# Order of the loads and of the second layer's preparation at the head of a Mamba and attention megakernel

## Chip, cores and metric

The kernel runs on one core of one Trainium2 chip. The metric is the time of one execution on the device in microseconds (us); lower is better. Everything is fp32.

## The reference, cut to what matters

The program is a chain of four image layers on x of shape (2, 128, 64, 64). The change touches the first layer and the preparation for the second.

```python
def layer0(x, ...):                       # two Mamba + FFN blocks over 4096 tokens of 128 channels
    t = tokens(embed_w @ x + embed_b)
    for i in range(2):
        r = t
        t2 = layernorm(t, ln_g[i], ln_b[i])
        u, z = split(t2 @ in_w[i].T)
        u = silu(causal_conv4(u, conv_w[i]) + conv_b[i])
        dt, Bm, Cm = split(u @ xproj_w[i].T)
        dt = softplus(dt @ dtproj_w[i].T + dtproj_b[i])
        A = -exp(A_log[i])                # (256, 16)
        # h_t = exp(dt*A) * h_{t-1} + dt*u*Bm ;  y_t = h_t . Cm + u*ssm_D
        t = ((y * silu(z)) @ mout_w[i].T) + r
        t = t + ffn(layernorm(t))         # gelu FFN, 4x wide
    return x + outc_w @ t + outc_b
# layer 1: q, k, v by 3x3 convolutions, softmax attention over 4096 positions, 1x1 convolution, + x
# layer 2: attention with 1x1 q, k, v;  layer 3: 3x3 convolutions at four scales, attention over the scales
```

## The kernel before

**The tiling.** Layer 0 is cut into 32 items: image b (2) times block l (2) times chunk c (8 chunks of 512 tokens). Each item has 8 steps (`NST`) of the scan, each step holds 4 state rows for 128 partitions, and a period of 32 slots (`NSL`) belongs to each item. The loop at L514 runs over periods i = -2 to 33. In each slot it issues, in a fixed order, the scan of item i with what feeds it (`spread_dt`, `spread_dtu`, `y_pair`, `scan`, `decay`, `times_b`, L350 to L402) and then what `background(i)` has listed for the slot (L463): for item i+2 the embedding and first layer norm, for item i+1 the projection (`pu_taps`, `xproj`, `spread_bc`, `dtproj`, `soft_plus`), for items i-1 and i-2 the output and the FFN. Periods -2 and -1 have no scan of their own: they fill the pipeline.

**What sets the order.** The order is written out by hand: each engine runs its instructions in the order in which the program issues them (`tc.manual_schedule`). SyncE (SP) issues nearly all DMAs in this order on one queue. DMA completions are counted on eight semaphores used in turn, so an issue also waits until the DMA eight places before it has landed.

**The head.** SP issues, in this order: `kc` (constants, L76), `vec` (L77), the eight chunks of image 0 (L93), `we` (embedding weights, L121), then for both blocks `wl` (L139), `cw` in two parts (L141 the four convolution taps spread over all partitions, L142 the input projection), and `wd` (L144), then the three `raw` convolution weights of layer 1 (L163) and the eight chunks of image 1 (L166).

The other engines prepare both blocks one after the other (L146 to L159): four VectorE (DVE) products `wu` of the projection with each tap (L148), `an = -exp(A_log)` on ScalarE (ACT) and DVE (L150, L151), and four TensorE (PE) matmuls `pa` (L155) that spread `an` over partitions, each followed by four small DVE copies into `am` (L158). Only then does period -2 begin with `embed` of chunk 0 (L213).

`pa` takes its PSUM from the pool `mm` (two buffers, L114), as do `pe`, `pc`, `var`, `pr`, `pu`, `pd`, `pt` and others. `pu` of one half keeps its buffer from its first tap (slot 0 of the period) to `pu_out` (slot 2).

**Period -1** (around the change): `pu_taps` for item 0 at slots 0, 1, 3 and 4 (four taps for each half of the 256 inner channels, two in each slot), `fold(k)` for k = 0, 1, 2 at slots 2, 10 and 18 (L490), `silu` at slot 11, `xproj` 13, `spread_bc` 14, `soft_plus` 17, the first `spread_dt` at slot 20. `fold` (L168) is ten DVE operations that make transformed weights for layer 1 out of `raw`, and two DMA stores to `ufold` in DRAM (L184), which are read again only after layer 0. `cw`, `raw`, `ulo`, `uhi` and the scan's `h` share one tag of five SBUF buffers.

`spread_bc` (L323) stores rows of `dbl` to DRAM (L326) and reads them back spread over partitions, as `bb` and `cb`, 256 KB in each of eight DMAs (L331). `spread_dt` (L350) makes `dtb` for one step with four DMAs of 64 KB (L355); `decay` (L368) needs it, and `scan` (L375) needs `decay`.

Of the kernel before, what the change touches and what calls it, by code (L numbers as in the profile page):

```python
# [6 lines left out]
F32 = mybir.dt.float32  # L7
AF = mybir.ActivationFunctionType
ALU = mybir.AluOpType
# [4 lines left out]
B, C, H, W = 2, 128, 64, 64  # L14
N = H * W
P = 128
CH = 512
NCH = N // CH
RPC = CH // W
NL = 2  # L20
DS = 16
DI = 2 * C
# [3 lines left out]
KC = 4  # L26
# [41 lines left out]
def tile_conv_seq(ctx: ExitStack, tc, x, consts, vecs, wemb, wlay, wconv, wdt, wqkv, wsmall, wms, out):  # L68
    nc = tc.nc
# [9 lines left out]
    def xv(b, c):  # L79

        return xt[:, b, 1 + c * RPC : 1 + (c + 1) * RPC, 1 : W + 1]
# [7 lines left out]
        nc.gpsimd.memset(xt[:, b, 1 : H + 1, 0:1], 0.0)  # L89
        nc.gpsimd.memset(xt[:, b, 1 : H + 1, W + 1 : W + 2], 0.0)  # L90

    for c in range(NCH):
        nc.sync.dma_start(xv(0, c), x[0, :, c * RPC : (c + 1) * RPC, :])  # L93

    ud = ctx.enter_context(tc.tile_pool(name="ufold", bufs=1, space=bass.MemoryType.DRAM))
    ufold = [ud.tile([P, 18, C], F32, name=f"ufold{k}") for k in range(3)]
# [14 lines left out]
    with ExitStack() as s, tc.manual_schedule():  # L111
        wp = s.enter_context(tc.tile_pool(name="l0w", bufs=1))
        sp = s.enter_context(tc.tile_pool(name="l0s", bufs=1))
# [18 lines left out]
        def four(g):  # L132
            return fsel[:, g].rearrange("p q d -> p (q d)")

        nc.scalar.preload_act_table_set(EXP_LN_SET)
        wl, wu, wd, am = [], [], [], []
        for l in range(NL):
            w = wp.tile([P, NWL - DI], F32, name=f"wl{l}")
            nc.sync.dma_start(w, wlay[l][:, DI:])  # L139
            cw = sp.tile([P, KC + 1, DI], F32, name="cw", tag="h", bufs=5)  # L140
            nc.sync.dma_start(cw[:, :KC, :].rearrange("p k d -> p (k d)"), wconv[l : l + 1, :].to_broadcast([P, KC * DI]))  # L141
            nc.sync.dma_start(cw[:, KC, :], wlay[l][:, :DI])  # L142
            d = wp.tile([R, DI], F32, name=f"wd{l}")
            nc.sync.dma_start(d, wdt[l])  # L144

            u = wp.tile([P, KC, DI], F32, name=f"wu{l}")  # L146
            for k in range(KC):
                nc.vector.tensor_tensor(u[:, k, :], cw[:, KC, :], cw[:, k, :], ALU.mult)  # L148
            an = wp.tile([P, NJ * DS], F32, name=f"an{l}")
            nc.scalar.activation(an, vec[:, VEC[f"A_log{l}"] : VEC[f"A_log{l}"] + NJ * DS], AF.Exp)  # L150
            nc.vector.tensor_scalar(an, an, -1.0, None, ALU.mult)  # L151
            a = wp.tile([P, NJ, 4, 4], F32, name=f"am{l}")
            for g in range(4):
                pa = mm.tile([P, NJ, DS], F32, name="pa", tag="mm")
                nc.tensor.matmul(pa.rearrange("p j n -> p (j n)"), lhsT=four(g), rhs=an, start=True, stop=True)  # L155
                for q in range(4):
                    at = slice(32 * q, 32 * q + 32)
                    nc.vector.tensor_copy(a[at, :, g, :], pa[at, :, 4 * q : 4 * q + 4])  # L158
            wl.append(w), wu.append(u), wd.append(d), am.append(a)  # L159
        raws = []  # L160
        for which in range(3):
            raw = sp.tile([P, 3, 3, C], F32, name="raw", tag="h", bufs=5)
            nc.sync.dma_start(raw.rearrange("p y x c -> p (y x) c"), wqkv[:, which])  # L163
            raws.append(raw)
        for c in range(NCH):
            nc.sync.dma_start(xv(1, c), x[1, :, c * RPC : (c + 1) * RPC, :])  # L166

        def fold(which):  # L168

# [26 lines left out]
        def has(i):  # L196
            return 0 <= i < NI
# [265 lines left out]
        def background(i):  # L463

            todo = [[] for _ in range(NSL)]

            def at(t, f, *a):
                todo[t].append((f, a))

            n, p, q, r = i + 1, i - 1, i - 2, i + 2  # L470
            if has(q):
                at(3, gelu, q)
                at(6, ffn_down, q, (0, 1)), at(7, ffn_down, q, (2, 3)), at(9, ffn_add, q)
                at(11, out_mm, q), at(12, out_add, q)
            if has(p):
                at(7, y_out, p, 1), at(7, gate, p)
                at(9, mix_out, p), at(11, mix_add, p)
            if has(n):
                at(0, pu_taps, n, 0, (0, 1)), at(1, pu_taps, n, 0, (2, 3)), at(2, pu_out, n, 0)
                at(3, pu_taps, n, 1, (0, 1)), at(4, pu_taps, n, 1, (2, 3)), at(5, pu_out, n, 1)  # L480
                at(13, xproj, n), at(14, xproj_out, n), at(14, spread_bc, n)
                at(15, dtproj, n, 0), at(16, dtproj, n, 1), at(17, soft_plus, n), at(18, dt_end, n)
            if has(i):
                at(1, pz_mm, i, 0), at(3, pz_out, i, 0)
                at(5, pz_mm, i, 1), at(6, pz_out, i, 1)
            if has(i) or has(n):
                at(11, silu, i, n)
            if i == -1:
                for k in range(3):
                    at(8 * k + 2, fold, k)  # L490
            pair = [(k, second) for k, second in ((p, True), (r, False)) if has(k)]
            if has(r):
                at(10, embed, r), at(11, embed_out, r)
            w, m = {}, len(pair)
            for k, (it, second) in enumerate(pair):
                at(12 + 2 * k, ln_centre, w, k, it)
                at(13 + 2 * k, ln_square, w, k, it)
                at(27, ln_spread, w, k, m), at(28, ln_scale, w, k, it)
                at(29, ln_shift, w, k, it, second)
            if pair:  # L500
                at(17, ln_var, w, m), at(18, ln_eps, w, m), at(19, ln_rs, w, m), at(20, ln_newton, w, m), at(21, ln_step, w, m)
            if has(p):
                for f in range(4):
                    at(30 + f // 2, ffn_up, p, f)
            if has(i):
                at(24, y_out, i, 0)
            return todo
# [6 lines left out]
        for i in range(-2, NI + 2):  # L514
            todo = background(i)
            for t_ in range(NSL):
                t = i * NSL + t_
                g, m = divmod(t, 4)
                if m == 0 and 0 <= g + 3 < NG:
                    spread_dt(g + 3)  # L520
                if m == 0 and 0 <= g + 1 < NG:
                    spread_dtu(g + 1)
                if m == 0 and g % 2 == 1 and 0 <= g - 3 < NG:
                    y_pair(g - 3)
                if 0 <= t < NT:
                    scan(t)
                if 0 <= t + 4 < NT:
                    decay(t + 4)
                if m == 3 and 0 <= g + 1 < NG:
                    times_b(g + 1)  # L530
                for f, a in todo[t_]:
                    f(*a)
# [14 lines left out]
    with ExitStack() as s, tc.manual_schedule():  # L547
        sp = s.enter_context(tc.tile_pool(name="ats", bufs=1))
# [259 lines left out]
        for now in range(NALL + LAG + 10):  # L808
            r, u = divmod(now, NU)
            w = now % 8  # L810
# [56 lines left out]
    with ExitStack() as s, tc.manual_schedule():  # L867
        sp = s.enter_context(tc.tile_pool(name="mss", bufs=1))
# [50 lines left out]
        for si in (2, 3):  # L919
            wgt[si] = sp.tile([P, SCALES[si]], F32, name=f"wgt{si}")  # L920
            for k in range(SCALES[si]):
                w = (k + 0.5) / SCALES[si] - 0.5
# [398 lines left out]
```

## Time and profile before

| | |
|---|---|
| median of 3 runs | 5102.76 us |
| lowest, highest | 5097.54, 5103.26 us |
| profiled execution, its own time | 5104.57 us |
| its span | 5102.8 us |
| mean granted TensorE clock | 0.946 |
| PE, DVE, ACT, POOL busy | 92%, 80%, 46%, 45% of the span |
| first embedding matmul (`pe`, L213) | 28.91 us after the span's start |
| first projection matmul (`pu`, L288) | 46.34 us |
| first `dtb` DMA issued (L355) | 74.15 us |
| first scan (L384) | 84.72 us |

Times in the views are counted from the start of the span. "DMA x<-y" in the chain of waits is the time from an issue to its landing; "issue" is time in which the engine waited for nothing that the profile shows. SPq is SyncE's queue. PEld is TensorE's loading of weights. A matmul of the program is two instructions on PE in fp32, so "x16" for `pu` is eight taps.

### The profile page before, as it was taken

The page shows a single profiled execution, that of the slowest core. Times are in us where ns is not written, and L with a number is a line of the kernel's source. Part 1 is how long each engine was busy: PE and PEld are TensorE (multiplying, and loading weights), DVE is VectorE, ACT ScalarE, POOL GpSimd, SP SyncE. Part 2 cuts the span into 40 slices and gives each one's busy share as a digit, 9 for nine tenths or more (in the row PEclk, how much of TensorE's full clock was granted, in tenths as well). Part 3 has the DMA queues.
Part 4 walks back from the last instruction along what each step waited for, and adds up shares of the span by engine and source line. Part 5 has one row for each costly group of instructions (what it writes and reads, how often), then busy time and mean ns, then how long its engine had stood idle before and what let it go on. Part 6 is the DMA issues. An engine that isn't in the chain of part 4 may idle for free.

```text
span 5102.8 us, 48990 instructions
## 1 busy us (share of the span) xinstructions
PE 4686.2 (92%) x14797; PEld 2249.2 (44%) x14797; DVE 4094.2 (80%) x4416; ACT 2367.7 (46%) x3221; POOL 2317.8 (45%) x1948
## 2 busy tenths in 40 slices
PE   5888899899888998789999999999999998999997
PEld 1222222222222222256666666666666666333332
DVE  5999999999999999588888887667766775667775
ACT  4677777777777777412222232333333332323332
POOL 2777777666777777313332233333333332322331
PEclk8899998998999989899999999999999999999998
DMA  5333333332333333124443344444444443000000
GB/s 150 73 68 68 70 71 72 71 70 68 69 69 68 69 71 72 36 53 104 101 105 82 78 100 105 118 95 112 111 99 97 112 111 76 3 7 5 7 8 7
DMA packets 237016, 373.86 MB, mean 73 GB/s; under 512 B 88000, under 2 KB 88400, under 8 KB 228432
## 3 DMA queue, kind: packets, MB, share of 16 engines
q1 hardware_dynamic: 187600, 303.55, 25.0%
q10 hardware_dynamic: 49152, 67.17, 5.5%
q8 instruction: 118, 1.93, 0.2%
q14 instruction: 146, 1.20, 0.1%
HBM read 92.18 MB, written 9.83 MB: 20 GB/s over the span
## 4 chain that ended last, share of the span: by engine, by line
PE 46%; POOL 21%; DVE 13%; issue 11%; DMA 4%; ACT 3%; SPq 3%; DVEq 0%; ACTq 0%; POOLq 0%
POOL h L387 17%; PE po L756 13%; PE pq L706 13%; DVE tr L736 3%; DMA pt<-tr 2%; SPq L747 2%; PE pf L1008 2%; PE py L399 2%; PE pqkv L1035 2%; PE pw L1094 1%; POOL dtu L347 1%; POOL z L410 1%; PE pfus L1159 1%; PE pu L288 1%; PE psc L1059 1%
## 5 line engine op out<-in xcount | busy, mean ns | idle before, releaser
L743 POOL COPY pt<-tr 32x512 f32<-32x512 f32 x1024 | 657.8, 642 | 1496.0 <-DVE tr L736 769.0
L384 DVE TENSOR_TENSOR_SCAN h<-da,carry,h 128x512 f32<-128x512 f32 x1024 | 1240.9, 1265 | 60.1 <-ACT da L373 29.9
L387 POOL TENSOR_TENSOR h<-h,cb 128x2048 f32<-128x2048 f32 x256 | 1161.0, 4535 | 20.9 <-POOL carry L386 0.2
L706 PE MATMUL pq<-k,q 128*128 128x512 f32 x2048 | 966.5, 595 | 11.0 <-DVE sc L711 8.7
L756 PE MATMUL po<-pt,vt 128*128 128x256 f32 x4096 | 965.6, 379 | 2.5 <-DMA pt<-tr 2.5
L721 ACT ACTIVATE sc<-sc,nm 128x2048 f32<-128x2048 f32 x256 | 510.6, 1995 | 938.9 <-DVE nm L717 651.9
L711 DVE TENSOR_SCALAR_CACHE_REDUCE sc<-pq 128x1024 f32<-128x1024 f32 x512 | 625.0, 1222 | 361.3 <-PE pq L706 339.7
L756 PEld LDWEIGHTS po<-pt,vt 128*128 128x128 f32 x4096 | 777.9, 190 | 294.8 <-issue 211.4
L373 ACT ACTIVATE da<-dtb,am 128x512 f32<-128x512 f32 x1024 | 681.6, 684 | 223.8 <-DVE h L384 212.0
L736 DVE STREAM_TRANSPOSE tr<-sc 128x2048 f32<-128x2048 f32 x256 | 591.7, 2311 | 68.3 <-DMA pt<-tr 61.4
L366 DVE TENSOR_TENSOR h<-bb,pdu 128x2048 f32<-128x2048 f32 x256 | 581.3, 2271 | 78.4 <-PE py L399 29.4
L399 PE MATMUL py<-h,sel 128*32 128x512 f32 x2048 | 512.1, 644 | 1.6 <-POOL h L387 1.6
L706 PEld LDWEIGHTS pq<-k,q 128*128 128x128 f32 x2048 | 384.4, 191 | 291.3 <-issue 248.0
L360 PE MATMUL pdu<-dtu,fsel 128*128 128x512 f32 x512 | 324.3, 719 | 104.3 <-DVE h L366 104.2
L399 PEld LDWEIGHTS py<-h,sel 128*32 128x32 f32 x2048 | 115.4, 118 | 415.0 <-issue 407.9
L288 PE MATMUL pu<-xn,wu 128*128 128x512 f32 x512 | 246.1, 614 | 4.1 <-ACT xn L278 2.3
L360 PEld LDWEIGHTS pdu<-dtu,fsel 128*128 128x128 f32 x512 | 95.6, 213 | 309.8 <-DVE h L366 190.5
L386 POOL COPY carry<-h 128x4 f32<-128x4 f32 x256 | 47.8, 187 | 390.3 <-DVE h L384 386.4
L1101 DVE TENSOR_TENSOR ov<-v,pw 128x2048 f32<-128x2048 f32 x64 | 146.2, 2285 | 68.6 <-PE pw L1094 68.6
L1035 PE MATMUL pqkv<-f,ws 128*128 128x512 f32 x384 | 189.5, 618 | 3.0 <-DVE prod L1052 2.3
L1105 POOL TENSOR_TENSOR ov<-ov 128x2048 f32<-128x2048 f32 x16 | 72.6, 4537 | 257.6 <-DVE ov L1101 257.6
L261 PE MATMUL pr<-rs,kc 2*128 2x512 f32 (+1 forms) x128 | 90.2, 834 | 77.3 <-POOL rs L257 71.1
(241 smaller groups left out, 5331.8 us busy)
## 6 DMA issues: line engine op xcount, KB each, us to landing
pt<-tr SPq DMA_DIRECT2D x2048, 64.0 KB, 2.0
dtb<-dt SPq DMA_DIRECT2D x1024, 64.0 KB, 2.0
pt<-tr ACTq DMA_DIRECT2D x1024, 64.0 KB, 2.2
bb<-dr SPq DMA_DIRECT2D x128, 256.0 KB, 4.6
cb<-dr SPq DMA_DIRECT2D x128, 256.0 KB, 7.5
uw<-ufold SPq DMA_DIRECT2D x14, 576.0 KB, 3.9
xt<-in_x SPq DMA_DIRECT2D x16, 256.0 KB, 5.0
xr<-in_x SPq DMA_DIRECT2D x16, 256.0 KB, 2.9
```

Source lines behind the costliest of these rows:

```text
L360: nc.tensor.matmul(pdu, lhsT=four(s_ % 4), rhs=st[i]["dtu"][:, s_ // 4, :], start=True, stop=True)
L366: nc.vector.tensor_tensor(h, st[i]["bc", 0], pdu.unsqueeze(1).to_broadcast([P, 4, CH]), ALU.mult)
L373: nc.scalar.activation(da, st[i]["dtb", s_], AF.Exp, scale=am[items[i][1]][:, j, gg, m : m + 1])
L384: nc.vector.tensor_tensor_scan(h[:, m, :], da, h[:, m, :], carries[b, l][:, j, gg, m : m + 1], ALU.mult, ALU.add)
L387: nc.gpsimd.tensor_tensor(h, h, st[i]["bc", 1], ALU.mult)
L399: nc.tensor.matmul(py[r : r + 32, :], lhsT=sel, rhs=st[i]["h", s_ + k][:, m, :], start=(m == 0), stop=(m == 3), tile_position=(0, r),)
L706: nc.tensor.matmul(pq[:, i, :], lhsT=st["q", r, grp][:, it * P : (it + 1) * P], rhs=st["k"][:, at : at + CH], start=True, stop=True)
L711: nc.vector.tensor_scalar(dst, pq, 1.0, None, ALU.mult, ALU.max, accum_out=st["mx"][:, c2 : c2 + 1])
L721: nc.scalar.activation(sc, sc, AF.Exp, bias=nm, scale=scale, accum_out=sm[:, hh : hh + 1])
L736: nc.vector.transpose(tr, st.pop(("sc", r, blk, hh)).rearrange("p (t r f) -> p r t f", r=NB, f=32))
L743: nc.gpsimd.tensor_copy(dst, src)
L756: nc.tensor.matmul(st["po", r, grp], lhsT=st["vt"][:, jt, :], rhs=rhs, start=(jt == 0), stop=(jt == N // P - 1))
```

## The change

At the head, the loads are put in the order of use: `kc`, `vec`, `we`, chunk 0 of image 0, block 0's weights with `cw` first, then chunks 1 to 7 of image 0, block 1's weights, `raw`, image 1. Block 1's preparation (`prepare(1)`: `an`, the four `pa` with their copies, and the four products `wu`) moves out of the head to slot 0 of period -1, where it is issued just after the first two taps of `pu` for item 0. The loads of `raw` and of image 1 are issued from slot 1 of period -1, and `fold` moves from slots 2, 10, 18 to 6, 14, 22. Inside `prepare`, `an` and `am` come before `wu`. Nothing else differs, and no operation is added or removed.

On SP, the order of instructions differs in two places only: the loads at the head, and in period -1, where the two stores of `fold(1)` now stand after `cb` and ahead of the first `dtb`, and those of `fold(2)` between the four DMAs of the first `dtb` and those of the second. Before, `fold(0)` and `fold(1)` stood ahead of `dr`, and `fold(2)` between `cb` and the first `dtb`.

```diff
-    for c in range(NCH):
-        nc.sync.dma_start(xv(0, c), x[0, :, c * RPC : (c + 1) * RPC, :])
+    def load_x(b, c):
+        nc.sync.dma_start(xv(b, c), x[b, :, c * RPC : (c + 1) * RPC, :])
...
         nc.scalar.preload_act_table_set(EXP_LN_SET)
-        wl, wu, wd, am = [], [], [], []
-        for l in range(NL):
+        load_x(0, 0)
+        wl, wu, wd, am, cws = [], [], [], [], []
+
+        def load_layer(l):
+            cw = sp.tile([P, KC + 1, DI], F32, name="cw", tag="h", bufs=5)
+            nc.sync.dma_start(cw[:, KC, :], wlay[l][:, :DI])
+            nc.sync.dma_start(cw[:, :KC, :].rearrange("p k d -> p (k d)"), wconv[l : l + 1, :].to_broadcast([P, KC * DI]))
+            cws.append(cw)
             w = wp.tile([P, NWL - DI], F32, name=f"wl{l}")
             nc.sync.dma_start(w, wlay[l][:, DI:])
-            cw = sp.tile([P, KC + 1, DI], F32, name="cw", tag="h", bufs=5)
-            nc.sync.dma_start(cw[:, :KC, :].rearrange("p k d -> p (k d)"), wconv[l : l + 1, :].to_broadcast([P, KC * DI]))
-            nc.sync.dma_start(cw[:, KC, :], wlay[l][:, :DI])
             d = wp.tile([R, DI], F32, name=f"wd{l}")
             nc.sync.dma_start(d, wdt[l])
-
-            u = wp.tile([P, KC, DI], F32, name=f"wu{l}")
-            for k in range(KC):
-                nc.vector.tensor_tensor(u[:, k, :], cw[:, KC, :], cw[:, k, :], ALU.mult)
+            wl.append(w), wd.append(d)
+
+        def prepare(l):
             an = wp.tile([P, NJ * DS], F32, name=f"an{l}")
...
-            wl.append(w), wu.append(u), wd.append(d), am.append(a)
+
+            u, cw = wp.tile([P, KC, DI], F32, name=f"wu{l}"), cws[l]
+            for k in range(KC):
+                nc.vector.tensor_tensor(u[:, k, :], cw[:, KC, :], cw[:, k, :], ALU.mult)
+            wu.append(u), am.append(a)
+
         raws = []
-        for which in range(3):
...
-        for c in range(NCH):
-            nc.sync.dma_start(xv(1, c), x[1, :, c * RPC : (c + 1) * RPC, :])
+
+        def load_rest():
+            for which in range(3):
+                raw = sp.tile([P, 3, 3, C], F32, name="raw", tag="h", bufs=5)
+                nc.sync.dma_start(raw.rearrange("p y x c -> p (y x) c"), wqkv[:, which])
+                raws.append(raw)
+            for c in range(NCH):
+                load_x(1, c)
+
+        load_layer(0)
+        load_x(0, 1)
+        prepare(0)
+        for c in range(2, NCH):
+            load_x(0, c)
+        load_layer(1)
...
             if i == -1:
+                at(0, prepare, 1), at(1, load_rest)
                 for k in range(3):
-                    at(8 * k + 2, fold, k)
+                    at(8 * k + 6, fold, k)
```

More of the change, by code (lines that the diff above doesn't have):

```diff
@@ L158, in tile_conv_seq @@
                     nc.vector.tensor_copy(a[at, :, g, :], pa[at, :, 4 * q : 4 * q + 4])
-            wl.append(w), wu.append(u), wd.append(d), am.append(a)
+            u, cw = wp.tile([P, KC, DI], F32, name=f"wu{l}"), cws[l]
+            for k in range(KC):
+                nc.vector.tensor_tensor(u[:, k, :], cw[:, KC, :], cw[:, k, :], ALU.mult)
+            wu.append(u), am.append(a)
         raws = []
-        for which in range(3):
-            raw = sp.tile([P, 3, 3, C], F32, name="raw", tag="h", bufs=5)
-            nc.sync.dma_start(raw.rearrange("p y x c -> p (y x) c"), wqkv[:, which])
-            raws.append(raw)
-        for c in range(NCH):
-            nc.sync.dma_start(xv(1, c), x[1, :, c * RPC : (c + 1) * RPC, :])
+        def load_rest():
[11 more added lines that the diff above has]
+        load_layer(1)
         def fold(which):
```

## Prediction

> **What bounds the kernel now.** I read the page first, for the whole, and then the head alone, because the change ends there: the last instruction that it moves lies within the first 90 us.
>
> ```profile
> span 5102.8 us, 48990 instructions
> PE 4686.2 (92%) x14797; PEld 2249.2 (44%) x14797; DVE 4094.2 (80%) x4416; ACT 2367.7 (46%) x3221; POOL 2317.8 (45%) x1948
> ```
>
> The reader is to see that over the whole span TensorE and VectorE are full. No operation is removed, so the change can only shorten the filling of the pipeline. Whether such a saving lasts is a question of elasticity: after the first scan, every wait in the trace is for another engine or a DMA of the same pipeline, none for a fixed time, so an earlier first scan moves all that follows. The exception is the granted clock of TensorE (mean 0.946).
>
> Second, the chain of waits, asked for the first 95 us (start, length, what):
>
> ```profile
> 11.61 0.43 SPq L141
> 12.08 7.01 DMA cw<-in_wlay
> 19.19 1.43 DVE wu L148 x4
> 20.62 0.10 DVE an L151
> 20.77 0.65 PE pa L155 x2
> ...
> 24.34 1.43 DVE wu L148 x4
> ...
> 28.20 0.62 PE pa L155 x2
> 28.82 0.09 issue
> 28.91 2.06 PE pe L213 x2
> ...
> 46.34 9.89 PE pu L288 x16
> 56.26 0.69 ACT u L294
> ...
> 66.62 1.60 DMA dr<-dbl
> 68.24 0.32 SPq L331
> 68.61 4.29 DMA bb<-dr
> 72.97 9.85 DMA ufold<-uhi
> 82.83 0.51 SPq L355
> ```
>
> The head is a single file. Until 12 us SP issues loads, the last part of `cw` lands at 19.09, both blocks are prepared one after the other, and the first embedding starts only at 28.91, although its own inputs were issued by 11. From `pe` on, layer norm, projection and `dbl` follow without a gap; then DMAs follow in one queue.
>
> Third, the waits of the first 90 us (us in total, times, longest):
>
> ```profile
> ACT xt L217 <- PE pe L213: 26.7, 1, 26.7
> DVE wu L148 <- DMA cw<-in_wlay: 14.6, 1, 14.6
> ACT da L373 <- DMA dtb<-dt: 8.4, 1, 8.4
> ```
>
> The first scan (84.72) is freed by `da`, which waited 8.4 us for the first `dtb`, landed at 83.9. So the path that sets the start is: preparation, `pe`, `pu`, `dbl`, `dr`, the DMA queue, `dtb`, `da`, scan.
>
> [...]
> - [...] weight loads of `pu` are 0.86 us apart until 51.60 and 0.43 from 52.19, 5.8 us after the matmuls began.
> - [...] In the trace `pe` stands behind the last `pa`, though its inputs are there.
> - [...] the last `ufold` store, issued at 72.97 behind `bb` and `cb`, took 9.85 us, where the median is 2.8.
>
> **The change, part by part.**
>
> *Loads.* `kc` and `vec` stay first and land at 3.65 and 3.91. `pe` now needs `we` and chunk 0, 767 KB with what is ahead of them. In slices of 2.5 us the trace shows 76 and 257 GB/s, 0.83 MB by 5.0 us; or a chunk issued at 2.05 with the median 5.0 us to land gives 7.05. I take 5 to 7. `cw` of block 0 ends at 1407 KB, some 8 us at the next slice's 226 GB/s (estimate), and `pu` needs it at 25: free. SP's bytes up to image 1 are unchanged, so `raw` lands near 24 and image 1's issues end near 32, as now; their cover is that `dbl` is ready only after 50.
>
> *Preparation of block 0.* DVE finishes `fsel` at 4.56 (start 3.94, 0.62), `an` is then 0.17 with a 0.1 gap, and the first `pa` starts at 4.83. From `pa` to `pe` I take block 1's stretch before: 26.00 to 28.91, 2.91. So `pe` starts at 7.74, if chunk 0 is there; it is 0.7 to 2.7 us earlier. The gain so far is 28.91 - 7.74 = 21.2 us. `wu` (1.43) comes after `am` on DVE at about 8.5 to 10, hidden by the layer norm (DVE waits for `pr` there).
>
> *`pe` to `pu`.* Unchanged and cold, 46.34 - 28.91 = 17.43. `pu` starts at 25.2.
>
> *Preparation of block 1, now between the taps.* PE has four `pa` after taps 0 and 1 and ahead of taps 2 and 3. `pu` holds one `mm` buffer through them, so all four `pa` go through the other, and each waits for the copies of the one before. Before, they had two buffers and overlapped. One turn: matmul to first copy 0.65, four copies 0.70 (21.44 to 22.14), back to PE 0.14, together 1.49. Three turns, the last `pa` 0.62 and 0.09 give 5.2 us in which taps 2 and 3 wait. Behind them on PE is everything: the second half's taps, `pe` of item 1, `xproj`. `an` is no delay: ACT's exponential (0.18) and DVE's 0.17 end within taps 0 and 1 (3.44). On DVE the copies end near 34.5, `wu` near 36, and the three folds (15.3 together, 45.36 to 60.63) near 51.5; the next DVE work that the path needs is `cen` (79.03 before, about 65 after). That slack of 13 us covers prepare and folds.
>
> *The clock.* Before, `pu`'s 16 instructions took 9.88. After, four run cold before the `pa` (3.44), and 12 after. If warming starts anew there and takes the same 5.7 us, 6.6 of them are cold: 12 x 0.43 + 6.6 x 0.43 + 0.16 = 8.2. The second half then ends at 25.2 + 3.4 + 5.2 + 8.2 = 42.0, where it ended at 56.22: 14.2 us earlier. Bounds: all 12 warm, 5.3, gain 17.1; all cold, 10.5, gain 11.9.
>
> *`dbl` to scan.* Same instructions, 14.2 us earlier: `dr` at 52.4. SP has nothing waiting ahead: `fold(0)` is done by about 41.
>
> *Stores of `fold`.* Two stores of 576 KB stand between `cb` and the first `dtb` before and after, only of `fold(1)` in place of `fold(2)`. `fold(1)` is ready near 46.4, SP reaches it near 57.7. So the first `dtb` keeps its 17.3 us behind `dr`: no gain. `fold(2)`'s 1.15 MB now go ahead of the second `dtb`. At the 393 to 404 GB/s of the trace's slices with `ufold` stores that is 2.9 us; in times of before the second `dtb` lands near 87.5. The second scan step starts at 91.81, after DVE's first four scans and `times_b`, and needs one `da` of 0.69: slack 3.5. Free, and without that slack it costs at most 2.9.
>
> *Sum.* -21.2 + 5.2 + (3.4 + 8.2 - 9.88 = 1.7) = -14.2 (rounded parts differ by 0.1). Against the profiled execution, 5104.6 (span and 1.8 around it), that is 5090.4; this execution is 1.8 above the median of the runs, so from the median 5102.8 it gives 5088.5. The runs before spread over 5.7 us; about 0.2%, 10.2 us, is what can be told from no change.
>
> **Rivals.**
>
> *A: the `pa` chain hides, or counts as activity and PE stays warm.* For it: `pa` occupies PE some 40% of each turn; against: the trace shows PE cold at 28.91 right behind such a chain. Gain 17 to 21.2; I price it at 19, 5083.8.
>
> *B: part is lost on the way.* Chunk 0 lands after 7.7, PE stays cold through all taps and `xproj`, or the second `dtb` is late by 2.9. For it: the backlog of loads at the head is continuous; against: the slack above in each place. All cold 11.9, less 2.9 gives a gain of 9, 5093.8.
>
> *C: slower, SP blocked by a fold.* The stores of `fold(1)` now stand ahead of the first `dtb`; SP waits there for DVE, and DVE for `prepare(1)` and `raw`. It decides once `fold(1)` ends later than SP arrives (57.7, slack 11.3), then 1 us per us; beyond 25.5 us of lateness the kernel is slower than before, and by 0.2% at 35.7. At 40 us late: 5102.8 - 14.2 + 28.7 = 5117. Nothing in the profile makes `fold` so late: `raw` had landed long before its first use at 45.36.
>
> *That the change doesn't do what it says:* the instruction streams show exactly these moves and no others, and the `pa` of block 1 with a wait for DVE on each after the first. I give it nothing of its own.
>
> **How the numbers follow.** Forecast 62% (gain 11.9 to 17.1), A 17%, B 18%, C 3%. Faster by over 0.2% holds the forecast and A and a part of B (about 4 of 18): 83%; same 14%; slower 3%. The range of 8 in 10 takes the bounds of the clock with 3 us for the median's scatter and reaches into A and B: 5082 to 5095.
>
> **What would show it right or wrong.** In the new profile `pe` should start near 7.7 and `pu` near 25.2; four `pa` about 1.5 us apart should lie inside `pu`; `dr` should be issued near 52.4, the first `dtb` near 60 and the first scan near 70.5. From there the whole should be shifted by 14. If `pe` comes later, chunk 0 or `we` was late; if `pu`'s stretch is not near 16.9, the clock or the buffers were misjudged; if the first scan is 14 us earlier and the end is not, the pipeline took it back, and my step that nothing there waits for a fixed time is wrong.

## The result, and the profile after

The changed kernel takes 5083.2 us (median of 7 runs, 5081.95 to 5087.57) against 5101.19 before (7 runs, 5097.54 to 5103.26). The ratio is 0.9967, with a 95% interval of 0.9956 to 0.9978. It is faster by 18.0 us in the medians and by 21.4 in the two profiled executions (5104.57 and 5083.2, spans 5102.8 and 5081.4). 14.2 had been forecast. The whole kernel looks as it did:

```profile
span 5081.4 us, 48993 instructions
PE 4682.7 (92%) x14797; PEld 2249.1 (44%) x14797; DVE 4094.3 (81%) x4416; ACT 2367.7 (47%) x3221; POOL 2316.2 (46%) x1948
```

The same work, nearly the same busy time (TensorE's is 3.5 us less), a shorter span: the engines wait less somewhere. Where, the chain of waits of the first 80 us says (start, length, what). This is the changed kernel; lines of the code that the change pushed down have numbers 2, 16 or 17 higher than before.

```profile
4.68 0.65 PE pa L157 x2
...
7.62 2.06 PE pe L229 x2
...
25.05 3.75 PE pu L304 x4
28.80 0.28 PE pa L157 x2
29.62 0.18 DVE am L160
29.94 0.62 PE pa L157 x2
31.10 0.18 DVE am L160
31.42 0.62 PE pa L157 x2
32.58 0.18 DVE am L160
32.90 0.61 PE pa L157 x2
33.51 7.22 PE pu L304 x12
40.74 0.69 ACT u L310
...
51.95 1.61 DMA dr<-dbl
```

`cw` has gone from the chain, and `pe` starts at 7.62, 21.3 us earlier. Layer norm follows without a gap until `pu` at 25.05. Then the moved preparation shows: a `pa` of 0.62 every 1.48 us, each behind the copies (`am`) of the one before, and only then the other twelve instructions of the taps. `dr` is issued at 51.95, where it was 66.62.

The waits of the first 75 us (us in total, times, longest) show what took the place of the old ones:

```profile
ACT u L310 <- PE pu L304: 15.0, 2, 12.1
...
ACT da L389 <- DMA dtb<-dt: 9.0, 2, 8.4
...
ACT xt L233 <- PE pe L229: 5.7, 1, 5.7
```

ACT's wait for the first `pe` fell from 26.7 to 5.7, VectorE's 14.6 for `cw` is no longer among the long ones, and `da` still waits 8.4 for the first `dtb`. New is 12.1 for the second half of `pu`.

I read the same points in both traces, all in us:

| point | before | after | difference |
|---|---|---|---|
| first `pe` starts | 28.91 | 7.62 | -21.29 |
| first `pu` starts | 46.34 | 25.05 | -21.29 |
| second `u` on ACT (first item's taps are done) | 56.26 | 40.74 | -15.52 |
| first `dr` issued | 66.62 | 51.95 | -14.67 |
| first scan | 84.72 | 70.03 | -14.69 |
| last `dr` (end of layer 0) | 2014.18 | 1999.59 | -14.59 |
| from there to the end ("the rest") | 3088.62 | 3081.81 | -6.81 |

Two questions follow. Of 21.3 us gained at `pe`, 6.6 are lost again before `dr`: to what? And why do 6.8 more come in layers 1 to 3, where no instruction has changed?

### The profile page after: what moved, and what is told of

Its sections match the earlier page's. It is cut to its first block, busy times and chain, and to the rows that moved or that the text cites. A ratio compares the mean times of both kernels' runs of the same rounds, so it can differ in the third digit from the quotient of the medians.

```text
span 5081.4 us, 48993 instructions
## 1 busy us (share of the span) xinstructions
PE 4682.7 (92%) x14797; PEld 2249.1 (44%) x14797; DVE 4094.3 (81%) x4416; ACT 2367.7 (47%) x3221; POOL 2316.2 (46%) x1948
## 4 chain that ended last, share of the span: by engine, by line
PE 46%; POOL 23%; DVE 12%; issue 11%; DMA 3%; ACT 3%; SPq 2%; DVEq 0%; ACTq 0%; POOLq 0%
POOL h L403 18%; PE po L773 14%; PE pq L723 14%; DVE tr L753 3%; PE pf L1025 2%; DMA pt<-tr 2%; SPq L764 2%; PE pqkv L1052 2%; PE py L415 1%; PE pw L1111 1%; POOL dtu L363 1%; POOL z L426 1%; PE pfus L1176 1%; PE psc L1076 1%; PE po L1132 1%
## 5 line engine op out<-in xcount | busy, mean ns | idle before, releaser
L389 ACT ACTIVATE da<-dtb,am 128x512 f32<-128x512 f32 x1024 | 681.5, 684 | 223.7 <-DVE h L400 208.6
L363 POOL TENSOR_TENSOR dtu<-dt,u 128x1024 f32<-128x1024 f32 x32 | 75.1, 2346 | 194.0 <-ACT dt L357 194.0
```

The source lines that it names most:

```text
L389: nc.scalar.activation(da, st[i]["dtb", s_], AF.Exp, scale=am[items[i][1]][:, j, gg, m : m + 1])
```

## The experiments

The first six kernels ask about the head, the others about the rest. In each, "the stretch" is from the start of the first `pu` to the second `u` on ACT (9.92 before, 15.69 after).

### The loads alone

Theory: the order of the loads and the move of the preparation are not two gains that add; each alone removes a different member of the same chain. This kernel has the new loads, but prepares block 1 in the head as before.

```diff
         load_layer(1)
+        prepare(1)
+        load_rest()
...
-                at(0, prepare, 1), at(1, load_rest)
                 for k in range(3):
-                    at(8 * k + 6, fold, k)
+                    at(8 * k + 2, fold, k)
```

> Only the new order of the loads; block 1 is still prepared in the head (its four pa ahead of pe), folds at slots 2, 10, 18. Theory: pe waits for both preparations, of which the first now ends at 8.3 us and wu of block 0 at 11.2 (cw lands at 9.8), so pa of block 1 starts near 11.4 and pe near 14.3; pu starts near 31.7 and, with no pa between its taps, ends near 41.6, against 40.7 in the changed kernel. So the first scan comes near 71 us, about 13.7 us earlier than before, and moving block 1's preparation is worth only about 1 us on top of the loads. Rival, that the two parts add up and the move is worth half of the gain: first scan near 77.

Measured: `pe` at 14.75, stretch 10.01, first scan at 70.57, 14.15 earlier than before; span 5088.8, time 5090.62 (one run) beside 5100.48 of the kernel before. The chain of waits of this kernel:

```profile
3.31 6.76 DMA cw<-in_wconv
10.16 1.43 DVE wu L164 x4
...
14.03 0.62 PE pa L157 x2
14.75 2.06 PE pe L231 x2
...
32.18 9.99 PE pu L306 x16
```

`cw` now lands at 10.07 and not at 19.09, but `pe` still stands behind eight `pa`, the second four of them behind VectorE's `wu` of block 0, which waits for this `cw` while block 1's `an` stands behind it on VectorE. The taps, on the other hand, run without a break. So with the loads alone the first scan comes within 0.54 us of the full change: the move of the preparation gave 7.1 us at `pe` and lost all but half a us of it in the taps.

### The move alone

```diff
+    for c in range(NCH):
+        load_x(0, c)
...
-        load_x(0, 0)
...
         def load_layer(l):
-            nc.sync.dma_start(cw[:, KC, :], wlay[l][:, :DI])
-            nc.sync.dma_start(cw[:, :KC, :].rearrange("p k d -> p (k d)"), wconv[l : l + 1, :].to_broadcast([P, KC * DI]))
             nc.sync.dma_start(w, wlay[l][:, DI:])
+            nc.sync.dma_start(cw[:, :KC, :].rearrange("p k d -> p (k d)"), wconv[l : l + 1, :].to_broadcast([P, KC * DI]))
+            nc.sync.dma_start(cw[:, KC, :], wlay[l][:, :DI])
...
-        load_x(0, 1)
         prepare(0)
-        for c in range(2, NCH):
-            load_x(0, c)
```

> Only the move of block 1's preparation (and of folds and later loads) to period -1; the loads stand in the old order. Theory: pa of block 0 is done by 7.6, but pe waits for we, which is issued behind all of image 0's chunk loads at 9.95 and lands near 13.5; wu of block 0 (cw lands at 19.1) is then still hidden. pu starts near 31, takes 15.7 with the pa between its taps, and ends near 46.6: first scan near 75, 9.6 us earlier than before. With e1 the two parts overlap: 13.7 and 9.6 for a sum of 14.7. Rival, that order of loads matters nothing once the preparation is moved: first scan at 70.

Measured: `pe` at 14.12, stretch 14.74, first scan at 75.32, 9.40 earlier; span 5093.6, time 5095.41 (one run). In its chain, the last load that `pe` needs stands behind the eight chunks of image 0:

```profile
8.91 1.22 SPq L93
10.18 3.81 DMA we<-in_wemb
...
14.12 2.06 PE pe L228 x2
```

The two parts alone give 14.15 and 9.40, which makes 23.55, and together 14.69. They share one chain; they are not a sum.

### The four `pa` in the layer norm's idle time

If the forecast's step "the `pa` stand in the taps" is the loss, the same four `pa` cost nothing where TensorE is idle, in the layer norm of item 0.

```diff
         def prepare(l):
+            prepare_am(l)
+            prepare_wu(l)
+
+        def prepare_am(l):
...
-                at(0, prepare, 1), at(1, load_rest)
+                at(1, load_rest), at(6, prepare_wu, 1)
...
+            if i == -2:
+                at(19, prepare_am, 1)
```

> The changed kernel, with block 1's an, pa and am put into the wait of the first layer norm (period -2, slot 19, behind var on TensorE) and its wu at slot 6 of period -1. Theory: TensorE and VectorE are idle there, so the four pa cost the path only ACT's exponential, 0.2 us; pu takes 9.9 us again in place of 15.7, and dr is issued near 46.4 in place of 51.95: first scan near 64.4, 20.3 us earlier than before; the whole 20 to 24 us less than before. Rival, that the 15.7 of pu is a matter of the clock and not of the pa: pu stays above 14 and the first scan near 69.

Measured: stretch 9.96, first scan at 62.90, 7.1 earlier than in the changed kernel and 21.8 earlier than before. Median 5078.35 (4 runs), ratio to before 0.9955 (0.9938 to 0.9971). Its chain:

```profile
15.72 0.12 ACT an L156
...
21.17 2.07 PE pr L283 x2
23.24 1.64 issue
24.88 9.93 PE pu L310 x16
...
45.20 1.60 DMA dr<-dbl
```

`pu` starts at 24.88, no later than after (25.05), so the `pa` are hidden. The rival, that the stretch of 15.7 is the clock's and not theirs, would have left it near there; it falls in that form. The clock has a share all the same: the granted clock rises at 30.55, 5.7 us after `pu` begins, and is still up when `pc` runs behind the taps, which takes 1.29 here and 2.07 in the changed kernel (`pd`, at half clock in both, 3.34 and 3.39). From the second `u` to `dr` it takes 10.36, as before; in the changed kernel it took 11.21.

### Four buffers for `pa`

Here the `pa` stay in the taps, but take buffers of another pool that is free at this point, so that they need not wait for each other's copies.

```diff
-                pa = mm.tile([P, NJ, DS], F32, name="pa", tag="mm")
+                pp, tg = (dap, "da") if l else (mm, "mm")
+                pa = pp.tile([P, NJ, DS], F32, name="pa", tag=tg)
```

> The changed kernel, with block 1's pa in the four PSUM buffers of da, idle then, in place of one free buffer of mm. Theory: no pa waits for the copies of the one before, so four take about 2.2 us in place of 5.2; pu's stretch is near 12.7 in place of 15.7 and the first scan near 67. Rival, that TensorE's time in pa itself or its clock makes the stretch: it stays above 14.5 and the first scan at 69 to 70.

Measured: stretch 9.94, first scan at 64.48, span 5079.7, time 5081.53 (one run). Both expectations of the stretch were too long. TensorE's timeline of this kernel (start, length, what, idle before):

```profile
25.02 3.75 PE L305 MATMUL pu<-xn,wu 128*128 128x512 f32 x4 [1.69 <-ACT an L152]
28.56 1.12 PE L158 MATMUL pa<-an,fsel 128*128 128x32 f32 x8
29.52 5.40 PE L305 MATMUL pu<-xn,wu 128*128 128x512 f32 x12
```

From start to start, four `pa` take 0.96 us here (28.56 to 29.52) and 4.73 in the changed kernel's timeline (28.59 to 33.32). The other twelve instructions take 5.40 instead of 7.39 and run at the full clock: it had risen at 28.86, behind the first four taps, and stays up to 39.10. So the 5.75 us by which the stretch is longer after than here are about 3.8 of waiting for the copies and 2.0 of clock. The clock's share varies from one execution to the next: in the second profile of the changed kernel (below) the clock rises at 29.07, much as here, but falls again at 32.48 with the pauses, and the twelve take 6.88.

### The stores of `fold` later

The stores of `fold(1)` and `fold(2)` are issued behind the third `dtb`, to see what stands behind the wait of 8.4 us for `dtb`.

```diff
-            for k, u in enumerate((lo, hi)):
+            folded[which] = (lo, hi)
+            if which == 0:
+                fold_out(which)
+
+        folded = {}
+
+        def fold_out(which):
+            for k, u in enumerate(folded[which]):
...
+                at(28, fold_out, 1), at(29, fold_out, 2)
```

> The changed kernel, with the four stores of fold(1) and fold(2) issued behind the third dtb (slots 28 and 29 of period -1) in place of around the first. Theory: the first dtb lands right behind cb, some 3 us earlier (near 66), but the first scan then waits for times_b, which ends at 68.7 because its pdu comes behind pr of item 1 on TensorE; so the first scan comes near 68.8, only 1.3 us earlier than 70.0. Rival, that the stores set the start one for one: first scan near 67 or less. Second rival, that they cost nothing: 70.0.

Measured: from `dr` to `da` 14.59 instead of 17.30, but from `dr` to the first scan 16.84 instead of 18.08: only 1.24 us. The wait for `dtb` is down from 8.4 to 5.7. The chain of this kernel names the next in line:

```profile
59.56 5.89 DMA dtb<-dt
65.45 2.28 DVE h L389
...
67.86 2.75 DVE h L407 x3
```

`dtb` has landed at 65.45; VectorE's product for the same scan (`h`, L389) runs from 65.44 to 67.73 and is late next. It does not read `dtb`, though the chain leads over it: it reads `pdu`, which in TensorE's timeline ends at 65.40, behind `pr` of item 1 (61.33 to 63.40). And what is gained here is hardly kept: first scan 2.17 earlier than after (0.93 of it there already at the first `dr`, ahead of any moved store), last `dr` 0.48. How it is taken back inside layer 0 I did not settle. Span 5079.1, time 5080.86 (one run) beside 5104.06.

### Both together

The edits of the last experiment and of the one with `pa` in the layer norm.

> Both: pa of block 1 in the first layer norm, and the stores of fold(1) and fold(2) behind the third dtb. Theory: the gains add, 5.6 and 1.3: first scan near 63.1, 21.6 us earlier than before, and the whole 21 to 25 us less than before (ratio 0.9955 or so). Rival, that an earlier first scan is taken back by something later that does not move (a DMA backlog, a fold on VectorE): first scan above 66 or the last dr of layer 0 less than 19 us earlier than before.

Measured: first scan at 60.39, 24.3 earlier than before; last `dr` 1990.14, 2.7 earlier than with the `pa` alone. Median 5077.0 (5 runs) beside 5104.06, ratio 0.9949 (0.9935 to 0.9962). Its interval overlaps widely with that of the `pa` alone. The profiles too leave little for the stores: of the 2.5 us at the first scan, 1.65 are there already at the first `dr` (43.55 beside 45.20), ahead of any moved store, because the clock came up at 27.86 and not at 30.55 and the stretch took 8.72 for 9.96. From `dr` to the first scan it takes 16.84 and 17.70, and these 0.86 us are what the stores can have given.

### Are the 6.8 us of the rest the program's?

The unchanged kernels were profiled once more, to see whether the rest is scatter between executions.

> The kernel before once more, unchanged, for a second profile. If the 6.8 us after layer 0 belong to the change, the part from the last dr to the end is 3088 to 3089 again. If it is scatter of single executions, it lies anywhere from 3080 to 3089; the first scan stays within 1 us of 84.7.

> The changed kernel once more, unchanged, for a second profile. Two theories of the part of the gain that comes after layer 0 (6.8 us between the two profiles, from the last dr of layer 0 to the end: 3088.6 before, 3081.8 after). If it belongs to the change, this part is 3081 to 3083 again. If it is scatter of single executions, it lies anywhere from 3080 to 3089, while the first scan stays within 1 us of 70.0 (the clock of TensorE in pu alone can move it) and layer 0 from first to last dr within 0.6 us of 1947.6.

| profile | stretch | first `dr` | last `dr` | rest | span |
|---|---|---|---|---|---|
| before | 9.92 | 66.62 | 2014.18 | 3088.62 | 5102.8 |
| before, again | 8.82 | 65.79 | 2012.41 | 3088.59 | 5101.0 |
| after | 15.69 | 51.95 | 1999.59 | 3081.81 | 5081.4 |
| after, again | 14.73 | 50.77 | 1998.14 | 3081.86 | 5080.0 |

The rest repeats within 0.05 us and differs by 6.8 between the programs, so between these profiles it is no scatter. What scatters is the head: the stretch moves by a us with nothing changed. Two profiles of each don't show that the rest is the same in every execution: the seven times of one kernel spread over 5.7 us before and 5.6 after, and where they differ was not profiled.

### Layers 1 to 3 with TensorE kept busy in two gaps

The instructions of the rest are the same, so I looked for stretches of them that differ in length. The projection's last eight matmul instructions before `pqq` come after a gap of 3.40 to 3.46 us, in which TensorE waits for `k`, and they take a different time in the two kernels. TensorE's timeline, the kernel before (two places):

```profile
3301.25 5.40 PE L634 MATMUL pp<-xt,wa 128*128 128x512 f32 x8 [3.44 <-ACT k L561]
...
3787.09 6.58 PE L634 MATMUL pp<-xt,wa 128*128 128x512 f32 x8 [3.40 <-ACT k L561]
```

The same two places after:

```profile
3284.44 6.57 PE L651 MATMUL pp<-xt,wa 128*128 128x512 f32 x8 [3.46 <-ACT k L578]
...
3770.05 3.72 PE L651 MATMUL pp<-xt,wa 128*128 128x512 f32 x8 [3.40 <-ACT k L578]
```

The same work costs 3.72, 5.40 or 6.57. The theory was that the clock sometimes drops in such a gap and sometimes not. The test adds work in the gap, twelve instructions whose result nobody reads; the rest of the computation is whole. The same edit was made to the kernel before and to the one after:

```diff
                 if runs[r][0]:
+                    if which == 1 and cc == 2:
+                        idle = psq.tile([P, QG], F32, name="idle", tag="q")
+                        for _ in range(6):
+                            nc.tensor.matmul(idle, lhsT=ident, rhs=kc[:, :QG], start=True, stop=True)
```

> The kernel before with six more matmuls (128x256, into PSUM that nothing reads) at the start of runs 2 and 3 of the attention, where TensorE otherwise waits 3.4 us for ACT to empty pp. They add work and change no other order. Theory of the clock: the 6.8 us after layer 0 come from whether TensorE falls to half clock in idle gaps of 2 to 3.5 us (eight pp take 5.40 and 6.58 us after two such gaps here, 6.57 and 3.72 in the changed kernel, for the same work). With the gap filled both take about 3.7: the part from the last dr of layer 0 to the end falls from 3088.6 by 1.7 + 2.9 to about 3084. Rival, a wait for data or instructions behind the eight pp: 3088.6 stays, or grows by the added 2.6 us each.

> The changed kernel with the same six added matmuls at the start of runs 2 and 3. Theory of the clock: only the first of its two gaps was cold (6.57), so the part after the last dr falls from 3081.8 by 2.9 to about 3079; the difference of the two kernels in this part shrinks from 6.8 to about 5 us, the rest lying at other gaps (starts of runs 0 and 1, transposes of v). Rival: 3081.8 or more.

The kernel before with the gap filled, TensorE's timeline:

```profile
3294.41 2.75 PE L646 MATMUL idle<-kc 128*128 128x256 f32 x12
3298.02 3.72 PE L634 MATMUL pp<-xt,wa 128*128 128x512 f32 x8 [0.86 <-ACT k L561]
...
3782.15 3.72 PE L634 MATMUL pp<-xt,wa 128*128 128x512 f32 x8 [0.81 <-ACT k L561]
```

The one after:

```profile
3279.23 2.75 PE L663 MATMUL idle<-kc 128*128 128x256 f32 x12
3282.83 3.72 PE L651 MATMUL pp<-xt,wa 128*128 128x512 f32 x8 [0.85 <-ACT k L578]
...
3765.60 3.71 PE L651 MATMUL pp<-xt,wa 128*128 128x512 f32 x8 [0.81 <-ACT k L578]
```

All four are short now. The rest falls from 3088.6 to 3081.82 in the kernel before (6.8, where 4.6 had been expected) and from 3081.8 to 3078.39 in the one after (3.4): both rests are shorter with added work, and the difference between them shrinks from 6.8 to 3.4, further than the 5 that had been expected. The eight instructions take 3.71 or 3.72 in both places of both kernels, as they did unfilled in the one place where the granted clock was 1.00 (3770.05). So the eight instructions owe their length to the clock after the gap. One run each: 5095.39 and 5079.06 beside 5104.58 of the kernel before.

But these two places are not half of the 6.8. Unfilled, they took 12.0 us together before (5.40 and 6.58) and 10.3 after (6.57 and 3.72), 1.7 apart. If the instructions of both kernels are matched one by one from the last `dr` on, three more places stand out that the edit does not touch. Before:

```profile
2764.36 4.39 PE L612 MATMUL pb<-dhi,uw 128*128 128x256 f32 x12 [2.32 <-DVE dhi L598]
...
3366.08 3.43 PE L634 MATMUL pp<-xt,wa 128*128 128x512 f32 x4
...
3852.09 1.97 PE L669 MATMUL pvt<-kc,vs 128*128 128x128 f32 x8 [3.16 <-ACT vs L561]
```

After:

```profile
2749.24 2.86 PE L629 MATMUL pb<-dhi,uw 128*128 128x256 f32 x12 [2.33 <-DVE dhi L615]
...
3350.43 1.89 PE L651 MATMUL pp<-xt,wa 128*128 128x512 f32 x4
...
3832.18 1.27 PE L686 MATMUL pvt<-kc,vs 128*128 128x128 f32 x8 [3.17 <-ACT vs L578]
```

In the table, each stretch runs from the instruction behind the gap to the start of the first one that is at the same speed again; beside it stand the gap ahead of it and the mean granted clock in it (1 is full, 0.5 half):

| stretch (start before, after) | gap, before and after | us before | us after | difference | clock before, after |
|---|---|---|---|---|---|
| `pb` (2764.36, 2749.24) | 2.32, 2.33 | 4.19 | 2.69 | 1.50 | 0.64, 1.00 |
| eight `pp`, first place of the test (3301.25, 3284.44) | 3.44, 3.46 | 5.25 | 6.40 | -1.15 | 0.67, 0.55 |
| `pvt`, `pp`, `pvt` (3365.15, 3349.50) | 2.81, 2.81 | 5.21 | 3.82 | 1.39 | 0.67, 1.00 |
| eight `pp`, second place of the test (3787.09, 3770.05) | 3.40, 3.40 | 6.43 | 3.56 | 2.87 | 0.55, 1.00 |
| `pvt`, `pp`, `pvt` (3852.09, 3832.18) | 3.16, 3.17 | 6.30 | 5.21 | 1.09 | 0.55, 0.67 |

These five make 5.7 of the 6.8; the other 1.1 lies in pieces below 0.4. With the two gaps filled, the first and the third stretch still differ between the kernels (by 1.7 and 1.4, between VectorE's instructions on either side) and the fifth no longer does, which leaves the 3.4. So 5.7 of the 6.8 are TensorE's clock: shown by the test in the two places of `pp`, read from the granted clock in the other three.

The gaps ahead of a stretch are equal in both kernels within 0.02 us, and the clock behind them is not. So the length of a gap does not decide here: one of 2.32 us was followed by the half clock before, one of 3.40 us by the full clock after. What differs is when the gap comes. In the traces of before and after, every change of the granted clock (162 and 158 of them) comes a whole multiple of 3.413 us after the one before, within 0.06 us. Worked out from these records, the seven gaps of the table that were followed by the half clock have 2.0 to 3.3 us within a single stretch of 3.413 us (a window), and the three that were not have at most 1.9. That is a reading of ten gaps: no run moved a gap and nothing else.

### The two edits of the head and the filled gaps

The edits of `pa` in the layer norm, of the later stores and of the twelve unread instructions stand together in one kernel.

> The version with pa of block 1 in the first layer norm and the stores of fold(1) and fold(2) behind the third dtb, with six matmuls more at the start of runs 2 and 3 of the attention that keep TensorE's clock up (their result is not read). Its two stretches of eight pp took 5.4 us each without them; with them 3.7 each is expected, so the part from the last dr of layer 0 to the end falls from 3083.8 to about 3080.4, and the whole from 5077.0 to about 5073.5; ratio to the kernel before about 0.994. If the gains of head and clock do not add, the whole stays at 5077 or above.

Measured: median 5073.5 (5 runs, 5071.58 to 5074.83) beside 5101.97, ratio 0.9944 (0.9931 to 0.9958). The rest was 3081.83, not the expected 3080.4, and the last `dr` 1990.27 where the two edits of the head alone had 1990.14: the two profiled executions differ by 1.8 us (spans 5072.1 and 5073.9), all of it in the rest. That the median is 3.5 lower, as expected, the profiles don't explain. It is the fastest of the kernels run, about 10 us below the change as it was made (5083.2), though its interval overlaps with that of the two edits of the head alone.

## Why the prediction was right, and where it was not

The direction, the time (5083.2 within 5082 to 5095, likeliest 5088.5) and the mechanism held. Point by point:

- *Loads and preparation of block 0.* Forecast `pe` at 7.74, measured 7.62. Chunk 0 and `we` were there, and the stretch taken from block 1's `pa` fitted.
- *`pe` to `pu`.* Forecast 17.43, measured 17.43.
- *Four `pa` in the taps.* Forecast a turn of 1.49 and 5.2 in all. Measured 1.48, and 4.7 from the first `pa` to the next tap. The form of the wait, one buffer and the copies between, is shown by the kernel with four buffers.
- *The clock.* Forecast 8.2 for the last twelve instructions, with 5.7 us of warming anew, an estimate from the single rise in the taps of before (5.6 to 5.8 us behind their start at 46.34: the granted clock at 51.92, the short spacing of the loads from 52.19). Measured 7.22: in the list of weight loads the long spacing (0.85) ends at 37.54, about 4.0 us after the taps resume.

```profile
36.02 0.34 PEld L304 LDWEIGHTS pu<-xn,wu 128*128 128x128 f32 x1 [0.52 <-issue]
36.87 0.34 PEld L304 LDWEIGHTS pu<-xn,wu 128*128 128x128 f32 x1 [0.52 <-issue]
37.54 0.19 PEld L304 LDWEIGHTS pu<-xn,wu 128*128 128x128 f32 x1 [0.33 <-issue]
37.97 0.19 PEld L304 LDWEIGHTS pu<-xn,wu 128*128 128x128 f32 x1 [0.24 <-issue]
```

  Here the clock's term of the sum was mis-sized by one us and the `pa` by half a one, while the first four instructions took 3.75 in the chain where I had 3.4: together 6.9 were forecast and 5.8 measured (15.69 - 9.92). 5.7 us was no constant: in the second profile of the kernel before the clock rose 3.4 us after the taps began (50.16 - 46.77). In the second profile of the changed kernel the stretch is 14.73, and it went another way. The clock rose at 29.07, as the `pa` began, and fell again at 32.48, so that two `pa` are short and the last one and the taps behind it are slow once more:

```profile
29.98 0.38 PE L157 MATMUL pa<-an,fsel 128*128 128x32 f32 x2 [0.87 <-DVE am L160]
...
32.48 0.61 PE L157 MATMUL pa<-an,fsel 128*128 128x32 f32 x2 [0.87 <-DVE am L160]
32.90 6.88 PE L304 MATMUL pu<-xn,wu 128*128 128x512 f32 x12
```

  So the last rise in the taps came at 37.34 in one execution and at 35.89 in the other, and the stretch differs by 1.0 us.
- *`dbl` to scan.* "Same instructions" was right, "same time" was not: 0.85 us more from the second `u` to `dr` (11.21 for 10.36), which my sum left out. Most of it is `pc`, 2.07 for 1.33: the clock had fallen at 44.17, in the gap of 4.29 us ahead of it. A clock that is up sooner is no cure for this: the kernel with four buffers, up at 28.86, has fallen by then too and takes 11.39, the one with `pa` in the layer norm, up at 30.55, has not and takes 10.36. This and the 1.1 above cancel, so that `dr` came at 51.95 with 52.4 forecast; that they did is luck.
- *Stores of `fold`.* Forecast: 17.3 from `dr` to `da`, and the second `dtb` free. Measured 17.30; SP reaches the stores of `fold(1)` at 57.25, long after they are ready, and the second `dtb` makes `da` wait 0.65 without moving the second scan (7.09 us after the first, before and after).
- *Sum.* Forecast -14.2. Measured -14.67 at the first `dr` and -14.59 at the last of 32: layer 0 passes the shift on (in the other kernels within one us). Rival A (TensorE stays warm) was wrong for this change: with the pauses the twelve instructions begin at half clock in both profiles, whether it had risen ahead of the `pa` or not. It is right for the kernel with four buffers, where the pauses are gone and the twelve take 5.40. The time alone, 5083.2, would have spoken for A (5083.8); the profile speaks against it. Rival B (parts lost) and C (SP blocked by a fold) did not happen.
- *What failed* is the step that an earlier first scan "moves all that follows" by the same amount. I had named the granted clock as the exception and put nothing on it. It was worth 6.8 us in the profiles, and about 3.4 in the medians if their layer 0 is that of the profiles (18.0 - 14.6), a quarter to a half of the forecast gain. So the direction, the head and the range held, and the end came out earlier than its mechanism gives, for a reason that the forecast had at nothing. That it made the kernel faster and not slower is nothing that I could have read from the profile of before.

What the profiles say of this exception goes a little further than the test. I took the last rise of the granted clock before the first item's taps end, and compared it with the last `dr` and the end:

| kernel | clock up | from there to the last `dr` | rest |
|---|---|---|---|
| before | 51.92 | 1962.26 | 3088.62 |
| before, again | 50.16 | 1962.24 | 3088.59 |
| loads alone | 37.97 | 1962.26 | 3088.57 |
| move alone | 42.73 | 1962.26 | 3088.61 |
| four buffers | 28.86 | 1965.67 | 3085.17 |
| after | 37.34 | 1962.25 | 3081.81 |
| after, again | 35.89 | 1962.25 | 3081.86 |
| before, gaps filled | 49.32 | 1962.26 | 3081.82 |
| both edits of the head, gaps filled | 28.02 | 1962.25 | 3081.83 |
| after, gaps filled | 35.73 | 1962.27 | 3078.39 |
| `pa` in the layer norm | 30.55 | 1962.25 | 3083.80 |
| both edits of the head | 27.86 | 1962.28 | 3083.76 |
| later stores | 36.40 | 1962.71 | 3079.99 |

In eleven of the 13 profiles layer 0 lasts 1962.24 to 1962.28 us from that rise, whatever the head did: 575 windows less 0.4, at the mean of 3.4133 us that the traces of before and after give (5051.7 us for 1480 windows before). With four buffers it is one window more; the later stores fall out of the pattern. So in all but that last kernel the last `dr` stands 0.4 us ahead of the end of a window. And in the first ten rows the rest differs in steps of 3.4 us: 3078.4, 3081.8, 3085.2, 3088.6. The step is one window of the granted clock in the traces of before and after. I read this as: the pipeline falls into step with these windows, and a change of the head moves it by whole windows later on. This does not hold everywhere: the last three rows lie off the steps. It is a reading of numbers, argued and not shown. Why a gap lies otherwise in its window after than before stays open, since both kernels enter the rest 0.4 us ahead of a window's end and have drifted apart by only 0.5 us at the first of the five stretches (750.18 and 749.65 us behind the last `dr`).

## What to carry to other kernels

At the head of a pipeline, find which member of the chain ends last after each edit: two edits that each remove a member do not add (14.15 and 9.40 gave 14.69). Work that is moved out of the head has to go where its engine is idle and not merely where its result is due: the four `pa` cost 5.8 us in the taps, and nothing in the layer norm. Expect some us, of either sign, from TensorE's clock after idle gaps (here gaps of 2.3 to 3.5 us, and between the two kernels -1.15 to 2.87 us for one stretch and 6.8 us in the whole rest), and put them into the range; where such a gap can be filled with work that nobody reads, try it.

## What the runs showed of the hardware

- Eight matmul instructions of 128x512 in fp32 took 3.72, 5.40 or 6.57 us after gaps that differ by 0.06 us (3.40 to 3.46). With twelve unread instructions in the gap (2.75 us) they took 3.72 in all four places, and the rest of both kernels was shorter with more work (by 6.8 and 3.4 us).
- Every change of TensorE's granted clock in the traces of before and after (162 and 158) comes a whole multiple of 3.413 us after the one before, within 0.06 us. A gap of 2.32 us was followed by the half clock in one kernel, one of 2.33 was not in the other.
- Small matmuls with pauses (0.62 busy in 1.48) neither brought the clock up nor, in the second profile, kept it up for more than one window (29.07 to 32.48); the twelve instructions behind them took 7.39 and 6.88. Behind the same matmuls without pauses they took 5.40.
- The same program, run twice, had a head that differed by 0.8 to 1.2 us at the first `dr`, while its layer 0 from the clock's rise agreed within 0.02 and its rest within 0.05.
